# Order edges on TensorE and ScalarE for the pieces of other stages in a selective scan

## The chip, the cores and the metric

The kernel runs on one core of a Trainium2 chip. The metric is the time of one execution in microseconds of the device. Three runs of the kernel before took 17821.96, 17850.22 and 17869.16 us; their median, 17850.22 us, is the time to compare with.

The names of the engines are those of the profile: PE is TensorE (matmuls; PEld its loads of weights), DVE is VectorE, ACT is ScalarE, POOL is GpSimd, and SP is the queue that issues the DMAs.

## The reference, cut to what matters

Four layers run one after the other on eight images of 56 x 56 positions with 128 channels, all in float32. Layers 0, 2 and 3 are deformable convolutions; the change does not touch them. Layer 1 is a "visual state space" block (SS2D). Of its forward pass this is what matters here:

```python
dt = jax.nn.softplus(dt + dt_projs_b[None, :, :, None])
A = -jnp.exp(A_logs).reshape(K, Di, N)

def step(h, t):
    dt_t, u_t, B_t, C_t = t
    h = h * jnp.exp(dt_t[..., None] * A) + (dt_t * u_t)[..., None] * B_t[:, :, None, :]
    y = jnp.einsum('bkdn,bkn->bkd', h, C_t)
    return (h, y)
...
_, ys = jax.lax.scan(step, h0, ts)
```

There are K = 4 directions (rows, columns, and both backwards), Di = 256 channels and N = 16 states per channel, and L = 3136 positions to scan. Ahead of the scan stand a layer norm, a projection, a 3 x 3 depthwise convolution with SiLU, and the projections that give dt, B and C. Behind it stand a second norm, a gate, a projection back to 128 channels and an MLP with GELU.

## The kernel before, in words

The layers run one after the other; the scan layer (class `Vss`) lies in the middle of the span. Its method `scans` writes the whole layer in one loop.

**Steps and units.** A step is one image, one direction and one quarter of the positions (784 of 3136): 8 x 4 x 4 = 128 steps, sixteen to an image. A step has 32 units: eight groups of 32 channels (`cg`) by four groups of 4 states (`sg`); a unit is a tile of 32 x 4 = 128 partitions by 784 positions. So there are 4096 units, and for each of them:

- `decay` (L1424): ACT writes dA = exp(dt * A) into PSUM. Two buffers, so a decay waits for the scan two units before it.
- `inputs` (L1434): DVE multiplies u = (dt * x) * B for three of four state groups; for the fourth POOL does it (L1430, tile `up`).
- the scan (L1537): DVE runs h = dA * h + u along the 784 positions.
- L1540: ACT keeps the last column of h for the next step.
- L1542: POOL multiplies hc = h * C, into one of six buffers.
- `add_sums` (L1456): PE sums hc over the states into `acc`, two units at a time, written three units later. `close_sums` (L1467) has ACT copy `acc` out, and `open_sums` (L1448) starts the next one.

Once per channel group, `spread` (L1418) has PE copy dt * x from SBUF into PSUM (tile `dtu`, one buffer) by a product with the identity: two matmuls, four rows in the trace. DVE's u reads it. The copy for the next group is written in the unit with sg = 1, right behind the `inputs` of sg = 2, the last reader on DVE of the old copy.

**Pieces of other stages.** Three generators are cut into pieces by `yield`, and the loop runs pieces of them between the units. `prepare` computes dt, B and C of the next step (matmuls L1324 and L1337; ACT's copies and activations L1326, L1338, L1339, L1341 and L1342; POOL's L1344 and L1346; DMAs to DRAM). It is advanced as `ready`, one piece in the units with sg = 1 and 2, just before the scan of that unit is written. `output_stage` (norm, gate, projection, MLP: L1244 to L1302) and `input_stage` of the next image (stats, norm, transposes L1149, convolution L1171 and L1178, SiLU L1181) wait in the deque `tasks`, and `advance(1)` runs one piece of the first of them at the end of each unit with sg = 1, 2 or 3. In the last four steps of all it runs one in every unit. All these stages share one PSUM bank, the tile `misc` with one buffer.

**What sets the order.** The program is written with a planner that gives each engine its list of instructions. Each engine then runs its list in order. The planner goes by the order of writing, but where the oldest instruction cannot run yet in its own picture of time, a younger one that can is put first. An order edge (`issue_after(ins)`) says that what is written inside its block on the engine of `ins` stands behind `ins` in that engine's list. It adds no wait and no semaphore. The kernel has such an edge already in `add_sums`, behind `last_spread`, which is the last written copy of dt * x. SP's and POOL's lists get no edge from it, since an edge binds the engine of `ins` alone.

The calls of the three generators are in the loop of `scans`: `next(ready, None)` at L1533 and `advance`, defined at L1400. In the first image's first steps a third one, `first` (the input stage of image 0), is advanced by itself; the change leaves it as it is.

Of the kernel before, what the change touches and what calls it, by code (L numbers as in the profile page):

```python
# [44 lines left out]
AF = mybir.ActivationFunctionType  # L45
# [73 lines left out]
SC, SR = 784, 14  # L119
# [14 lines left out]
NCG, NSG = DI // TC, NST // TS  # L134
# [898 lines left out]
class Vss:  # L1033
# [339 lines left out]
    def scans(self):  # L1373
        nc, w = self.nc, self.w
# [10 lines left out]
        def chunks_for(c):  # L1385
            return min(NLC, -(-SR * (c + 1) // RPC))
# [10 lines left out]
                self.fetch_row(state[0], x, g)  # L1397
        tasks = deque()

        def advance(count):  # L1400
            for _ in range(count):
                while tasks:
                    try:
                        next(tasks[0])
                        break
                    except StopIteration:
                        tasks.popleft()

        def on_pool(t):

            return order[t][1] == NSG - 1

        def spread(at, t):

            s, (cg, sg) = state[at], order[t]
            ps = s["dtu", cg] = self.pdtu.tile([128, 2, 512], F32, name="dtu", tag="dtu")
            for b in range(2):
                last = nc.tensor.matmul(ps[:, b, :SH], lhsT=self.net.ident, rhs=s["dt", cg][:, 1, SH * b : SH * (b + 1)], start=True, stop=True)  # L1418
            self.last_spread = last.ins

        def decay(at, t):
            (i, k, c), s, (cg, sg) = steps[at], state[at], order[t]
            da = s["dA", t] = self.pda.tile([128, 1024], F32, name="dA", tag="dA")
            nc.scalar.activation(da[:, :SC], s["dt", cg][:, 0], AF.Exp, scale=w["A"][:, k, NSG * cg + sg : NSG * cg + sg + 1])  # L1424

        def inputs(at, t):
            s, (cg, sg) = state[at], order[t]
            if on_pool(t):
                u = self.work.tile([128, SC], F32, name="up", tag="up", bufs=1)
                nc.gpsimd.tensor_mul(u, s["dt", cg][:, 1], s["b", sg])  # L1430
            else:
                u = self.work.tile([128, SC], F32, name="u", tag="u", bufs=2)
                halves = [v.rearrange("p (x e) -> p x e", x=2) for v in (u, s["b", sg])]
                nc.vector.tensor_mul(halves[0], s["dtu", cg][:, :, :SH], halves[1])  # L1434
            s["u", t] = u
# [40 lines left out]

        spread(*units[0])
        decay(*units[0])
        inputs(*units[0])
        st = ready = None  # L1480
        group, late = [], deque()
        zeros = self.zeros()
        for now, (at, t) in enumerate(units):
            (i, k, c), s, (cg, sg) = steps[at], state[at], order[t]
            forward = k < 2
            if t == 0:
                if at % NSC == 0:
                    st = self.prep.tile([128, NT], F32, name="st", tag="st", bufs=2)
                    nc.gpsimd.memset(st, 0.0)
                if at % (NDIR * NSC) == 0 and i + 1 < self.images:  # L1490
                    tasks.append(self.input_stage(i + 1))
                ready = iter(())
                early = at + 1 < NSC
                if at + 1 == NSC:
                    for _ in first:
                        pass
                if at + 1 < len(steps):
                    if steps[at + 1][0] > i:
                        self.load_xb(i + 1)
                    ready = self.prepare(state[at + 1], *steps[at + 1][1:])  # L1500
            if t % (2 * NSG) == 0:
                late.append((now + 5, open_sums, (at, t)))
            while late and late[0][0] <= now:
                _, do, args = late.popleft()
                do(*args)
            if sg == 1:
                to = divmod(NCG * at + cg + 2, NCG)
                if to[0] < len(steps):
                    self.fetch_dt(state[to[0]], to[1])
            if t in (3, 19):  # L1510
                next(zeros, None)

            for x, when in enumerate(((25, 28, 29, 30), (26, 29, 30, 31))):
                if t in when and at + 1 < len(steps):
                    self.fetch_row(state[at + 1], x, when.index(t))
            if now + 1 < len(units):
                decay(*units[now + 1])
                if not on_pool(units[now + 1][1]):
                    inputs(*units[now + 1])

                if sg == NSG - 3 and now + 3 < len(units):
                    spread(*units[now + 3])
            if now + 2 < len(units) and on_pool(units[now + 2][1]):
                inputs(*units[now + 2])
            if early and t < 16:
                for _ in range(3):
                    if self.made < chunks_for(c + 1):
                        next(first)
            if early and t == 15:
                while self.made < chunks_for(c + 1):  # L1530
                    next(first)
            if t >= 16 if early else sg in (1, 2):
                next(ready, None)  # L1533
            hh = self.work.tile([128, SC], F32, name="h", tag="h", bufs=3)
            step = 1 if forward else -1
            u, dA = s.pop(("u", t)), s.pop(("dA", t))
            nc.vector.tensor_tensor_scan(hh[:, ::step], dA[:, :SC][:, ::step], u[:, ::step], st[:, t : t + 1], ALU.mult, ALU.add)  # L1537
            if c != (NSC - 1 if forward else 0):
                last = SC - 1 if forward else 0
                nc.scalar.copy(st[:, t : t + 1], hh[:, last : last + 1])  # L1540
            hc = self.work.tile([128, SC], F32, name="hc", tag="hc", bufs=6)
            nc.gpsimd.tensor_mul(hc, hh, s["c", sg])  # L1542
            group.append((order[t], hc))
            if t % 2:
                late.append((now + 3, add_sums, (at, group)))
                group = []
                if t % (2 * NSG) == 2 * NSG - 1:
                    late.append((now + 5, close_sums, (at, t)))
            if not early and sg or (i == self.images - 1 and k == 2):
                advance(1)  # L1550
# [4 lines left out]
        while tasks:  # L1555
            advance(1)
# [82 lines left out]
```

## Time and profile before

| | us |
|---|---|
| median of three runs | 17850.22 |
| the profiled execution | 17839.74 |
| its span, first to last instruction | 17838.2 |
| scan stage, first to last scan | 2213 to 13404 |
| DVE busy, whole span | 15386.3 (86%) |
| PE busy, whole span | 13881.5 (78%) |
| POOL busy, whole span | 11758.9 (66%) |
| ACT busy, whole span | 10928.2 (61%) |
| PE's mean granted clock | 0.851 |

The groups of instructions of the scan stage that matter, each with count, busy time and mean: the scans are 3072 + 1024 with 5579.2 + 1876.7 us (1840 and 1833 ns each); hc on POOL 4096 with 7539.5 us (1874 ns); dA on ACT 4096 with 3741.9 us (915 ns); u on DVE 3072 with 2864.6 us (957 ns); the copies dtu on PE 4096 rows with 2028.2 us.

How to read it: a busy time is a sum over the whole span, where the scan stage stands between two stages with other limits, so it has to be read for that stretch alone. In the lists of waits a row says who waited for whom, with us in total, number of times, and the longest. In a timeline a row has its start, its duration, engine, line, operation, tiles (out <- in) and how many like instructions were merged; the brackets have the idle time of that engine before it, and what ended it. Matmuls in float32 leave two rows each.

### The profile page before, as it was taken

To read this page: it belongs to the slowest core of one execution; us is meant where nothing else is said; L and a number is where in the kernel's file an instruction comes from. 1 tells how busy PE (TensorE), PEld (TensorE's weight loads), DVE (VectorE), ACT (ScalarE), POOL (GpSimd) and SP (SyncE) were. 2 spreads that over 40 slices of the span, in tenths; PEclk is the share of its full clock that TensorE was granted. 3 is DMA by queue.
4 is the path that set the end of the run, shared out by engine and by line. 5 is a ranking of instruction groups with operands and counts; after the bars stand their busy time and mean duration, and the time that the engine had idled before them with its cause. 6 is when DMAs were issued, how large, how long until landed. Compare 5 with 4: busy or idle time off the path is not lost. (4 is left out here: it accounts for less than half of the span.)

```text
span 17838.2 us, 255485 instructions
## 1 busy us (share of the span) xinstructions
PE 13881.5 (78%) x90058; PEld 6881.4 (39%) x90058; DVE 15386.3 (86%) x17779; ACT 10928.2 (61%) x19607; POOL 11758.9 (66%) x6462
## 2 busy tenths in 40 slices
PE   5777788788788788788778878878776888777777
PEld 3555522232232233232223223223224666555555
DVE  8888488998998998998898899899996888888886
ACT  4666566566566566566666656656554666666666
POOL 2222189998998998998998999899992111122221
PEclk7788898899899899889888888989887888777778
DMA  7777544444343343343444344344434777777777
GB/s 211 211 204 206 165 153 154 172 169 150 143 159 141 139 163 137 139 165 137 143 162 143 137 158 144 140 155 150 148 134 134 199 198 199 196 210 193 209 196 176
DMA packets 1343087, 2961.69 MB, mean 166 GB/s; under 512 B 90960, under 2 KB 893716, under 8 KB 1327420
## 3 DMA queue, kind: packets, MB, share of 16 engines
q1 hardware_dynamic: 1341788, 2945.17, 52.9%
q8 instruction: 718, 11.76, 0.3%
q14 instruction: 581, 4.76, 0.1%
HBM read 2240.63 MB, written 866.92 MB: 174 GB/s over the span
## 5 line engine op out<-in xcount | busy, mean ns | idle before, releaser
L1542 POOL TENSOR_TENSOR hc<-h,c 128x784 f32<-128x784 f32 x4096 | 7539.5, 1874 | 640.9 <-DVE h L1537 387.9
L1537 DVE TENSOR_TENSOR_SCAN h<-dA,st,u 128x784 f32<-128x784 f32 x3072 | 5579.2, 1840 | 438.9 <-ACT dA L1424 243.2
L1424 ACT ACTIVATE dA<-dt,v_A 128x784 f32<-128x784 f32 x4096 | 3741.9, 915 | 842.2 <-DVE h L1537 827.7
L1456 PE MATMUL acc<-hc,v_sum 128*32 128x392 f32 x16384 | 3148.3, 542 | 103.9 <-POOL hc L1542 103.3
L1434 DVE TENSOR_TENSOR u<-dtu,b 128x784 f32<-128x784 f32 x3072 | 2864.6, 957 | 382.5 <-PE dtu L1418 378.4
L1418 PE MATMUL dtu<-dt,ident 128*128 128x392 f32 x4096 | 2028.2, 626 | 1081.9 <-issue 833.4
L760 POOL TENSOR_TENSOR ay<-hat,om 112x756 f32<-112x756 f32 (+2 forms) x192 | 504.6, 2628 | 2848.6 <-ACT hat L751 2309.7
L1537 DVE TENSOR_TENSOR_SCAN h<-dA,st,up 128x784 f32<-128x784 f32 x1024 | 1876.7, 1833 | 232.0 <-POOL hc L1542 208.6
L1430 POOL TENSOR_TENSOR up<-dt,b 128x784 f32<-128x784 f32 x1024 | 1908.1, 1863 | 79.5 <-DVE h L1537 47.1
L845 ACT COPY st<-pt 128x448 f32<-128x448 f32 (+1 forms) x2240 | 1177.4, 542 | 1201.1 <-PE pt L843 1194.6
L812 DVE TENSOR_TENSOR win<-win,patch 112x252 f32 (+2 forms) x3456 | 1686.4, 501 | 132.2 <-POOL win L803 32.5
L1540 ACT COPY st<-h 128x1 f32<-128x1 f32 x3072 | 582.6, 190 | 1985.3 <-DVE h L1537 1976.8
L843 PE MATMUL pt<-ident,sw 112*128 112x112 f32 (+2 forms) x8960 | 1600.6, 308 | 165.6 <-DMA sw<-skew 165.5
L1456 PEld LDWEIGHTS acc<-hc,v_sum 128*32 128x32 f32 x16384 | 762.0, 116 | 2485.3 <-issue 1656.6
L1418 PEld LDWEIGHTS dtu<-dt,ident 128*128 128x128 f32 x4096 | 860.1, 230 | 2150.6 <-issue 1365.5
L803 POOL MEMSET win<- 128x1820 f32 (+2 forms) x384 | 630.0, 1647 | 1298.4 <-DMA skew<-win 1111.2
L859 PE MATMUL yps<-st,xw 128*32 128x48 f32 (+5 forms) x35840 | 1075.2, 244 | 420.7 <-ACT st L845 414.6
L843 PEld LDWEIGHTS pt<-ident,sw 112*128 112x128 f32 (+2 forms) x8960 | 1113.4, 160 | 441.0 <-issue 156.8
L809 DVE TENSOR_TENSOR patch<-ay,hat 112x756 f32<-112x756 f32 (+2 forms) x1152 | 1225.3, 1070 | 39.5 <-POOL ay L760 36.6
L859 PEld LDWEIGHTS yps<-st,xw 128*32 128x32 f32 (+2 forms) x35840 | 754.1, 125 | 849.5 <-ACT st L845 501.0
L749 ACT ACTIVATE hat<-om,taps 112x252 f32<-112x252 f32 x1280 | 758.6, 730 | 277.2 <-DVE patch L809 261.4
L1448 PE MATMUL acc<-y,ident 128*64 128x392 f32 x1536 | 599.1, 780 | 348.6 <-ACT y L1467 269.5
(193 smaller groups left out, 19827.3 us busy)
## 6 DMA issues: line engine op xcount, KB each, us to landing
dt<-dds SPq DMA_DIRECT2D x1024, 784.0 KB
b<-rows SPq DMA_DIRECT2D x512, 392.0 KB
c<-rows SPq DMA_DIRECT2D x512, 392.0 KB
dds<-dd SPq DMA_DIRECT2D x256, 784.0 KB
sw<-skew SPq DMA_DIRECT2D x224, 812.0 KB
sw<-skew SPq DMA_DIRECT2D x224, 672.0 KB
sw<-skew SPq DMA_DIRECT2D x224, 588.0 KB
skew<-win SPq DMA_DIRECT2D x128, 560.0 KB
```

The costliest lines, as they stand in the source:

```text
L809: nc.vector.tensor_mul(patch[:n], bcast(a, 3, KX), bcast(b, 2, KY))
L812: self.last_add = nc.vector.tensor_add(to, to, patch[:n, NCB * p : NCB * (p + 1)]).ins
L843: last = nc.tensor.transpose(ps[:m, n * g : n * (g + 1)], sw[:n, g, p : p + m], self.net.ident[:n, :n])
L845: nc.scalar.copy(st[:m], ps[:m, : G * n])
L859: self.nc.tensor.matmul(yps[CG * g : CG * (g + 1), t0:t1], lhsT=xw[:m, k + part, CG * g : CG * (g + 1)], rhs=st[:m, at + t0 : at + t1], st ...
L1418: last = nc.tensor.matmul(ps[:, b, :SH], lhsT=self.net.ident, rhs=s["dt", cg][:, 1, SH * b : SH * (b + 1)], start=True, stop=True)
L1424: nc.scalar.activation(da[:, :SC], s["dt", cg][:, 0], AF.Exp, scale=w["A"][:, k, NSG * cg + sg : NSG * cg + sg + 1])
L1430: nc.gpsimd.tensor_mul(u, s["dt", cg][:, 1], s["b", sg])
L1434: nc.vector.tensor_mul(halves[0], s["dtu", cg][:, :, :SH], halves[1])
L1456: nc.tensor.matmul(acc[r : r + TC, :SH], lhsT=w["sum"], rhs=hc[:, SH * b : SH * (b + 1)], start=False, stop=sg == NSG - 1)
L1537: nc.vector.tensor_tensor_scan(hh[:, ::step], dA[:, :SC][:, ::step], u[:, ::step], st[:, t : t + 1], ALU.mult, ALU.add)
L1542: nc.gpsimd.tensor_mul(hc, hh, s["c", sg])
```

## The change

The pieces from `ready` and from `tasks` are now run inside two nested order edges, through a helper `behind`. What a piece writes on PE is put behind the copy of dt * x that was written last, and what it writes on ACT is put behind the decay that was written last; `decay` keeps that instruction for it. At sg = 1 the last written copy is the one of the next channel group, and the last written decay is that of the next unit. The loop in `advance` is rewritten to the same effect: an exhausted generator is dropped and the next one tried. What the pieces write on DVE, POOL and SP is bound by neither edge.

```diff
+        def behind(stream):
+            with self.tc.issue_after(self.last_spread), self.tc.issue_after(self.last_decay):
+                return next(stream, self)
+
         def advance(count):
             for _ in range(count):
-                while tasks:
-                    try:
-                        next(tasks[0])
-                        break
-                    except StopIteration:
-                        tasks.popleft()
+                while tasks and behind(tasks[0]) is self:
+                    tasks.popleft()
 
         def on_pool(t):
 
@@ -1421,7 +1421,7 @@
         def decay(at, t):
             (i, k, c), s, (cg, sg) = steps[at], state[at], order[t]
             da = s["dA", t] = self.pda.tile([128, 1024], F32, name="dA", tag="dA")
-            nc.scalar.activation(da[:, :SC], s["dt", cg][:, 0], AF.Exp, scale=w["A"][:, k, NSG * cg + sg : NSG * cg + sg + 1])
+            self.last_decay = nc.scalar.activation(da[:, :SC], s["dt", cg][:, 0], AF.Exp, scale=w["A"][:, k, NSG * cg + sg : NSG * cg + sg + 1]).ins
 
@@ -1530,7 +1530,7 @@
             if t >= 16 if early else sg in (1, 2):
-                next(ready, None)
+                behind(ready)
```

## The prediction

> **What bounds the kernel now.** First the windows of the span, cut at the first and the last scan. The change touches only the scan stage, from 2213 to 13404 us:
>
> ```profile
> 0.00:2213.00 2213.00, 1566.87 (x17883) 1176.05 (x17884) 1667.33 (x3408) 1290.00 (x2418) 408.50 (x239) 0.79 0.72 199
> 2213.00:13404.00 11191.00, 8898.43 (x31778) 3154.45 (x31778) 10148.66 (x7689) 6904.84 (x12124) 10440.65 (x5770) 0.89 0.42 149
> 13404.00:17839.00 4435.00, 3416.22 (x40401) 2550.93 (x40397) 3570.33 (x6683) 2733.38 (x5067) 909.79 (x454) 0.79 0.72 192
> ```
>
> The columns are the length, then busy us of PE, PEld, DVE, ACT and POOL, then the granted clock, DMA share and GB/s. In the middle row POOL is busy 93%, DVE 91%, PE 80%, ACT 62%: two engines are close to full, and 1042 us of DVE is idle. The list of waits of DVE in that stretch says what ended the idle time:
>
> ```profile
> DVE u L1434 <- PE dtu L1418: 378.4, 154, 48.6
> DVE h L1537 <- POOL hc L1542: 287.1, 261, 3.4
> DVE h L1537 <- ACT dA L1424: 246.2, 245, 5.0
> ```
>
> The change aims at rows one and three: 378 + 246 = 625 us, 3.5% of the span, is the most that two punctual producers could give. How much of it comes from a piece that stands too early in a queue is the question; two timelines show the kinds. On PE, the longest waits for dtu look like this one:
>
> ```profile
> 8233.81 5.05 PE L1171 MATMUL misc<-xn,v_tap 128*128 128x448 f32 x12
> 8238.79 0.85 PE L1456 MATMUL acc<-hc,v_sum 128*32 128x392 f32 x2
> 8239.56 1.58 PE L1418 MATMUL dtu<-dt,ident 128*128 128x392 f32 x4
> ...
> 8241.18 1.85 DVE L1434 TENSOR_TENSOR u<-dtu,b 128x784 f32<-128x784 f32 x2 [5.85 <-PE dtu L1418]
> ```
>
> Twelve rows of the input stage's convolution hold the copy up until DVE waits 5.85 us. But the code writes these matmuls before that copy, so no edge is drawn between them. On ACT, a piece that is too early:
>
> ```profile
> 5869.09 1.62 PE L1324 MATMUL misc<-xb,v_xproj 128*40 128x392 f32 x2
> ...
> 5870.74 0.48 ACT L1326 COPY dbl<-misc 40x392 f32<-40x392 f32 x1 [3.90 <-PE misc L1324]
> 5871.13 0.19 ACT L1540 COPY st<-h 128x1 f32<-128x1 f32 x1
> 5871.22 0.91 ACT L1424 ACTIVATE dA<-dt,v_A 128x784 f32<-128x784 f32 x1
> ...
> 5872.22 1.85 DVE L1537 TENSOR_TENSOR_SCAN h<-dA,st,u 128x784 f32<-128x784 f32 x1 [2.21 <-ACT dA L1424]
> ```
>
> The copy of dbl is written behind these decays and stands ahead of them; ACT waits 3.90 us at it for PE, and the scan loses 2.21 us.
>
> **The change part by part.** No instruction or DMA is added or removed; SP and POOL get no edge. What moves is the order on PE and ACT. I set the order of the instructions in the trace against the order in which the code writes them. Of the pieces from `ready` and `tasks`, 549 + 1132 matmul instructions stand on PE ahead of the copy that was written last before them, and 670 + 481 instructions on ACT ahead of such a decay. These alone are bound.
>
> *Edge on PE.* For each of 1023 copies I took the time from the end of the u that frees dtu to the end of the copy and summed what PE did in it. Pieces in the wrong order hold up 214 copies by 328 us in all, but DVE waits at only some of them, 22 us together: after the last u of a channel group DVE still has three scans (3 x 1.84 = 5.5 us) and the copy takes 1.5, so about 4 us are free. The 355 us of pieces that lie in the copies DVE does wait for stand in the written order. Gain 0 to 22 us.
>
> *Edge on ACT.* The same sum from the end of the scan that frees a decay's PSUM buffer: early pieces, run or waited for, hold up 295 decays by 280 us, and scans wait 37 us of it. Gain 0 to 37 us.
>
> Together 0 to 59; I take 30. The piece is not gone: the copy of dbl stands one decay later and still waits for its matmul at the head of ACT, and the next decay has only 0.9 us of slack (a scan of 1.84 less a decay of 0.92).
>
> *Levelling of `prepare`.* The largest displacements are of `prepare`: its L1324 stands a median of 69 us ahead of its copy, up to 263, a step being 79 to 100 us. Steps 9 to 13 of image 2 (images and steps counted from 0) show it, in the windows of the second product of `prepare` (L1346) alone; the columns are length, POOL busy us and count:
>
> ```profile
> 5855.10:5946.50 91.40, 4.47 (x2) 0.84 0.41 146
> 5946.50:6032.80 86.30, 8.32 (x4) 0.84 0.36 129
> 6032.80:6114.60 81.80, 3.71 (x2) 0.83 0.43 152
> 6114.60:6193.20 78.60, 0.00 (x0) 0.83 0.35 126
> 6193.20:6276.40 83.20, 3.71 (x2) 0.90 0.44 160
> ```
>
> Step 10 carries two prepares, step 12 none. With the edges each carries its own. Steps 10 to 12 sum to 246.7, and POOL is 100% busy in the first two, so three equal steps of 82 give nothing. Step 9 holds doubled matmuls (16 rows of L1324 where others have 8) beside the output stage, and DVE waits 6.4 us for dA and 3.3 for dtu in it; other steps with an output stage take 84. So 0 to 6 us per image, I take 5, for seven images 35. The last image, whose prepares run ahead from step 6 on, has steps of 88.1 and 87.2 against a level of about 82: 8 more. Sum 43; at most 7 x 6 + 11 = 53, and at worst a loss of 24, if step 12 rises to 82 in seven images and nothing falls.
>
> *What the new order puts behind.* A copy that waits for u now holds whatever was allowed past it: output-stage matmuls (L1285, L1297, L1262, L1264), transposes L1149, `prepare`'s, and behind these ACT's reads of `misc`, which is one bank: who holds it stops every other piece. The add_sums behind the copy free hc, for which POOL already waits 231 us. PE stands idle before a copy in 469 cases for 1051 us already, until a u ends. Upper end: the transposes feed the convolution, and if each of its 49 chunks in seven images comes late enough to make one more wait like the 5.85 above, 287 us. Lower end 0: most steps have the 4 us. The nearest row is that convolution matmuls themselves are hardly displaced (13 of 882), so I stay near the low end: one more wait of mean size (330 us without the first wait of 48.6, by 153: 2.2 us), per image, 15 us. On ACT the moved pieces are a median of under 1 us and follow the decay, where 1.8 us of each unit are free (11191/4096 = 2.73, less 0.92); cover gone, that is the stall above again.
>
> [...]
>
> **Sum.** -30 - 43 + 15 = -58 us. The profiled execution took 17839.74 (span 17838.2), so it would take 17,782; the median of the runs, 17,850.22, lies 10.5 above it, so I forecast 17,792.
>
> **The rivals.** About 0.3% (53 us) is what a measurement of this kernel can tell from no change; the three runs lie 47 apart.
>
> *A, no effect that can be told (17,797 to 17,903).* The long waits stand in the written order, POOL is 97 to 100% busy in eight of sixteen steps, and the levelled prepare costs where it saves. For it: only 22 of 330 us at dtu are from early pieces. Against: five steps per image change for certain.
>
> *B, slower.* Early pieces hurt little (22 us), late ones much (355 us), because a late piece is older than the next copy and goes first. If the edges turn early pieces into late ones in the six steps per image that hold the input stage (steps 3 to 8, 89 to 101 us against 84), each such step gets one more wait; at 3.1 us (the commonest of the long ones) to 5.85, on 6 x 7 = 42 steps, that is 130 to 246 us, less the 73 of gain: 17,907 to 18,023. It decides from 24 such waits on, where 3.1 us each eat the 73. For it: `misc` is one bank, PE is 82 to 90% busy in those steps. Against: pieces there already run two to four units later than written, so most edges bind nothing.
>
> *C, much faster.* Pieces that start right behind a copy have the whole 10.9 us (four units) until the next one, so the lumps of convolution come into phase too. If half of the 330 and 246 us goes, 288: 17,562. For it: only the phase of the lumps makes the waits. Against: nothing keeps a lump of 12 rows out of the way of the next copy.
>
> **How the numbers follow.** Forecast case 0.42 (own range 17,730 to 17,830, four fifths of its chance beyond 0.3%), A 0.22, B 0.30, C 0.06. Faster 0.34 + 0.06 = 0.40; same 0.08 + 0.22 = 0.30; slower 0.30. The range goes from 17,690, which leaves C out, to 17,940, which takes in the lower half of B and leaves out 0.12.
>
> **What would show it.** In the changed profile no L1326 or L1338 stands ahead of a decay written before it, and L1346 runs twice in each step but the last of all. The wait of the scan for dA falls from 246 to about 200; that of u for dtu moves by less than 30. Steps 9 to 13 take 416 instead of 421 us. If the wait of u for dtu rises above 420, or POOL's wait for PE's acc above 300, B is right. I am wrong if the steps with the convolution (3 to 8) change by more than 2 us each, in either direction: the order there would then have been remade by edges that I take for idle.

## The result, and the profile after

The changed kernel takes 17913.45 us (median of six runs, 17901.44 to 17933.17), the kernel before beside it 17841.35 us (six runs, 17819.69 to 17869.16). The ratio is 1.0041, with a 95% interval of 1.0028 to 1.0054: slower by 72 us. The forecast was 17,792, faster by 0.3%. The direction was wrong; the measured time lies inside the range, in the part that rival B had brought in.

Where the time came from is first read in the windows of the changed kernel, cut at its own first and last scan (length, busy us of PE, PEld, DVE, ACT and POOL, clock, DMA share, GB/s):

```profile
0.00:2213.00 2213.00, 1576.36 (x17889) 1180.38 (x17889) 1668.57 (x3408) 1290.90 (x2421) 406.53 (x240) 0.79 0.72 199
2213.00:13470.00 11257.00, 8956.48 (x31775) 3112.01 (x31776) 10143.58 (x7689) 6894.05 (x12121) 10461.80 (x5770) 0.90 0.42 148
13470.00:17902.50 4432.50, 3413.35 (x40399) 2552.55 (x40395) 3572.16 (x6683) 2731.52 (x5066) 911.23 (x454) 0.79 0.72 192
```

Ahead of the scan stage and behind it the stretches are as long as before (2213 and 4432.5 us, against 2213 and 4435). The scan stage, from its first scan to the end of its last, went from 11187.5 to 11255.7 us, so it holds all of the loss. DVE, the engine with the scans, has the same work in it (10148.66 before, 10143.58 now); what grew is its idle time. The waits of DVE in that stretch of the changed kernel (us in total, times, longest):

```profile
DVE u L1434 <- PE dtu L1418: 524.5, 193, 48.5
DVE h L1537 <- ACT dA L1424: 270.1, 234, 4.0
DVE h L1537 <- POOL hc L1542: 223.9, 196, 3.3
```

The two waits that the change aims at rose, that for dtu by 146 us (378.4 before) and that for dA by 24 (246.2). The wait for hc fell by 63. POOL's own row in the same stretch:

```profile
POOL hc L1542 <- PE acc L1456: 299.7, 179, 5.0
```

Before it was 230.9 us. The prediction gave two signs for rival B, and either was to do: the wait for dtu above 420 us, which it is, and POOL's wait for `acc` above 300, which it misses by a hair.

To place the loss, the scans were cut into steps (32 scans each) and the step times averaged over images 1 to 6. These are sums per image, in us, over three kinds of steps: those with an output stage only, those with the input stage, and those with `prepare` alone and what is left. Each row comes from one profiled execution, which need not lie at its kernel's median: that of `prepare` only lies 27 us above it, that of the smaller pieces without edges 31. The rows below the second belong to the experiments that follow.

| kernel | steps 13 to 2 | steps 3 to 8 | steps 9 to 12 | sum |
|---|---|---|---|---|
| before | 503.5 | 563.9 | 336.9 | 1404.3 |
| after | 505.6 | 574.1 | 332.0 | 1411.7 |
| edges on `prepare` only | 514.9 | 559.7 | 332.1 | 1406.7 |
| edges on the input stage only | 505.1 | 572.9 | 336.2 | 1414.2 |
| PE edge on the output stage only | 498.7 | 558.4 | 333.8 | 1390.9 |
| no edge, smaller pieces | 504.2 | 539.0 | 338.3 | 1381.5 |
| all edges, smaller pieces | 505.0 | 539.1 | 335.2 | 1379.3 |

From before to after: +2.1 in steps 13 to 2, +10.2 in steps 3 to 8, -4.9 in steps 9 to 12, so 6 x 7.4 = 44 us in six images; image 0 adds 15 and image 7 adds 9. That makes the 68 us of the stage. The two waits do not move alike: per image, u's wait for dtu rises by 10.9 us in steps 13 to 2 and by 7.0 in steps 3 to 8 (from 38.0 to 45.0), while the scan's wait for dA falls by 6.7 in the first and rises by 6.4 in the second (from 14.5 to 20.9). The 10.2 us of steps 3 to 8 thus stand at both.

The longest wait for dtu in one of these steps shows the first kind. The timeline of the changed kernel in step 6 of image 3:

```profile
7028.82 0.93 PE L1418 MATMUL dtu<-dt,ident 128*128 128x392 f32 x2
...
7029.58 4.67 PE L1171 MATMUL misc<-xn,v_tap 128*128 128x448 f32 x12
...
7034.09 0.82 PE L1418 MATMUL dtu<-dt,ident 128*128 128x392 f32 x2
...
7034.95 1.86 DVE L1434 TENSOR_TENSOR u<-dtu,b 128x784 f32<-128x784 f32 x2 [7.04 <-PE dtu L1418]
...
7037.21 0.64 ACT L1174 ACTIVATE pre<-misc,v_col 128x448 f32<-128x448 f32 x1 [7.40 <-PE misc L1171]
```

Two pieces of the convolution, twelve rows, stand between the halves of a copy. No edge forbids it: they were written before that copy. In the kernel before, u waits 3.2 us for dtu in step 6 on average, now 12.3.

### The profile page after: what moved, and what is told of

It is laid out like the page before. It is cut to its first block, busy times and chain, and to the rows that moved or that the text cites. A ratio compares the mean times of both kernels' runs of the same rounds, so it can differ in the third digit from the quotient of the medians.

```text
span 17902.5 us, 255375 instructions
## 1 busy us (share of the span) xinstructions
PE 13946.2 (78%) x90058; PEld 6844.9 (38%) x90058; DVE 15384.3 (86%) x17779; ACT 10916.5 (61%) x19607; POOL 11779.6 (66%) x6462
## 4 chain that ended last, share of the span: by engine, by line
PE 34%; DVE 18%; issue 15%; ACT 10%; POOL 9%; DMA 2%; DVEq 0%; SPq 0%; POOLq 0%; ACTq 0%
DVE h L1537 9%; PE acc L1456 7%; POOL hc L1542 6%; PE dtu L1418 5%; DVE u L1434 3%; PE misc L1171 3%; PE pt L843 2%; PE ps L902 2%; PE misc L1324 2%; PE acc L1448 2%; PE yps L859 2%; PE ps L911 2%; ACT hat L749 2%; DVE win L812 1%; ACT dA L1424 1%
## 5 line engine op out<-in xcount | busy, mean ns | idle before, releaser
L1456 PE MATMUL acc<-hc,v_sum 128*32 128x392 f32 x16384 | 3400.8, 539 | 98.3 <-POOL hc L1542 97.8
L1434 DVE TENSOR_TENSOR u<-dtu,b 128x784 f32<-128x784 f32 x3072 | 2865.6, 957 | 530.4 <-PE dtu L1418 524.5
L1418 PE MATMUL dtu<-dt,ident 128*128 128x392 f32 x4096 | 1982.1, 611 | 1453.8 <-issue 1327.3
L1418 PEld LDWEIGHTS dtu<-dt,ident 128*128 128x128 f32 x4096 | 823.7, 223 | 2529.7 <-issue 2017.6
```

The source lines that it names most:

```text
L1456: nc.tensor.matmul(acc[r : r + TC, :SH], lhsT=w["sum"], rhs=hc[:, SH * b : SH * (b + 1)], start=False, stop=sg == NSG - 1)
```

## The experiments

All of them use the helper of the change, with one or both edges, and differ in which generators go through it:

```diff
+        def behind(stream):
+            with self.tc.issue_after(self.last_spread), self.tc.issue_after(self.last_decay):
+                return next(stream, self)
```

Times are medians, differences are against the kernel before as measured beside each run, and intervals are of the ratio.

### Which edge, and which caller

PE's edge alone and ACT's edge alone, on all pieces:

```diff
-            with self.tc.issue_after(self.last_spread), self.tc.issue_after(self.last_decay):
+            with self.tc.issue_after(self.last_spread):
```
```diff
-            with self.tc.issue_after(self.last_spread), self.tc.issue_after(self.last_decay):
+            with self.tc.issue_after(self.last_decay):
```

> Only the edge on PE is left (behind the last written copy of dt * x), for prepare and tasks alike. Theory P (the PE edge turns early pieces into late ones, which the next copy then has to wait behind): all of the loss stays, 17,890 to 17,930, and u's wait for dtu stays above 450 us (524 with both edges, 378 before). Theory Q (the ACT edge holds the one bank misc until behind a decay, and that makes the pieces late): nearly nothing is lost, 17,820 to 17,860, and the wait for dtu falls back to 380 to 420.

> Only the edge on ACT is left (behind the last written decay). Theory P: no loss; the prepares of steps 9 to 12 are still levelled, since ACT reads every matmul of prepare, so about 30 us are won: 17,800 to 17,840, and u's wait for dtu is 330 to 400 us. Theory Q: the loss stays, 17,890 to 17,930, with the wait for dtu above 450.

Both edges, but on `prepare` alone, and on the deque `tasks` alone:

```diff
-                while tasks and behind(tasks[0]) is self:
+                while tasks and next(tasks[0], self) is self:
```
```diff
-                behind(ready)
+                next(ready, None)
```

> Both edges, but only around prepare; the pieces of tasks go as before. If the pieces of tasks (transposes, convolution, output stage) that are made late are what costs, this keeps the levelling of steps 9 to 12 (-5 us per image in the changed kernel) without the loss in steps 5 and 6: 17,790 to 17,840. If prepare's own pieces do it, it is slow like the changed kernel, 17,880 to 17,930.

> Both edges, but only around the pieces of tasks; prepare runs as far ahead as before. If the pieces of tasks made late cost it: 17,900 to 17,960 (the loss of steps 5 and 6 without the 35 us that the levelling saves). If prepare's do: 17,830 to 17,860.

| run | us | difference | ratio |
|---|---|---|---|
| PE edge, all pieces | 17881.09 | +33 | 1.0015 (1.0006 to 1.0024) |
| ACT edge, all pieces | 17840.94 | -7 | 0.9995 (0.9986 to 1.0004) |
| both, `prepare` only | 17850.58 | +3 | 1.0002 (0.9993 to 1.0011) |
| both, `tasks` only | 17868.91 | +21 | 1.0009 (1.0000 to 1.0018) |

None of the four times lies in a band that had been expected. PE's edge costs, ACT's edge does nothing that can be told. By its waits PE's edge alone does what theory P says: u's wait for dtu is 520.0 us in the stage (378.4 before, 524.5 with both edges). ACT's edge does do what the prediction says of it: without the first wait of the stage, the scan's wait for dA falls from 265 to 211 us and u's wait for dtu rises from 330 to 401, the two counted with the short stalls too. One wait went and another came. The parts do not add up to the whole: +33 - 7 and +3 + 21 are both about 25, and the whole is 60 to 72. That an edge changes the planner's list as a whole is the likely reason; it was not shown.

`prepare` alone shows the levelling: -4.8 us per image in steps 9 to 12, as in the changed kernel, and -4.2 in steps 3 to 8, but +11.4 in steps 13 to 2. There the pieces that used to run a step ahead now stand among the output stage's, and u waits 13.9 us per image for dtu (1.1 before). The changed kernel has this wait too, in step 0 of image 2:

```profile
5116.39 1.51 PE L1266 MATMUL misc<-yin,v_out 128*128 128x392 f32 x4
...
5117.94 0.48 ACT L1268 COPY x<-misc 128x392 f32<-128x392 f32 x1 [2.82 <-PE misc L1266]
...
5118.61 0.93 PE L1273 MATMUL misc<-x,v_center 128*128 128x392 f32 x2
...
5120.25 1.58 PE L1418 MATMUL dtu<-dt,ident 128*128 128x392 f32 x4
...
5121.87 0.97 DVE L1434 TENSOR_TENSOR u<-dtu,b 128x784 f32<-128x784 f32 x1 [3.20 <-PE dtu L1418]
```

The copy stands behind L1273, which needs ACT's L1268, which needs PE's L1266: a round trip between two engines stands in PE's list ahead of the copy. All three are the output stage's; yet with PE's edge on that stage alone (below) the wait is 2.7 us per image in these steps, so it takes `prepare`'s edges to bring it. How they do it was not followed. Steps 0 to 2 and 13 to 15 of the kernel before had 0.1 to 0.3 us of wait for dtu each, now they have 1.6 to 2.2.

### The two generators in `tasks` apart

First the changed kernel once more, then both edges on `output_stage` alone, then on `input_stage` alone. From here on `ready` goes without edges unless it is said:

```diff
-                while tasks and behind(tasks[0]) is self:
+                while tasks and (behind(tasks[0]) if tasks[0].__name__ == "output_stage" else next(tasks[0], self)) is self:
```

> The changed kernel itself once more, beside the variants and on their chip, since the sum of PE edge alone (+33 us) and ACT edge alone (-7 us) is far from the +72 of both. If the two edges add up, 17,865 to 17,885 here; if they make each other worse, 17,900 to 17,930.

> Both edges, only around the pieces of output_stage; input_stage and prepare as before. By the steps of the run with edges on tasks only, the steps that hold nothing but the output stage (13 to 15 and 0 to 2 of the next image) became 4.8 us per image shorter, and those of the input stage 8 us longer. If each is the work of its own stage's edges: 17,800 to 17,830, u's wait for dtu 320 to 360 us. If the two can't be told apart: 17,850 to 17,880.

> Both edges, only around the pieces of input_stage. If the loss in steps 5 and 6 comes from the input stage's own pieces (transposes and norm made late, so that the convolution comes in lumps at the next copy): 17,890 to 17,920, with steps 5 and 6 at 98 to 104 us against 95. If it comes from the output stage's pieces running on into them: 17,840 to 17,860.

And a choice made from the step times so far, with the output stage's edges always, those of `prepare` in steps 3 to 12, none for the input stage:

```diff
-                behind(ready)
+                behind(ready) if 3 <= at % (NDIR * NSC) <= 12 else next(ready, None)
```

> Edges only where the steps became shorter: output_stage always, prepare in steps 3 to 12 of each image, input_stage never. Per image -4.8 us in steps 13 to 2 (as with tasks only), -4.2 in steps 3 to 8 and -4.8 in 9 to 12 (as with prepare only), over some seven images, if these parts add: 17,745 to 17,790. If a change of order in one step class spoils the next: 17,830 to 17,870.

| run | us | difference | ratio |
|---|---|---|---|
| the changed kernel again | 17901.77 | +60 | 1.0038 (1.0024 to 1.0051) |
| output stage only | 17773.39 | -69 | 0.9962 (0.9948 to 0.9976) |
| input stage only | 17897.17 | +55 | 1.0031 (1.0019 to 1.0043) |
| chosen | 17783.44 | -59 | 0.9969 (0.9957 to 0.9981) |

This is the main result of the study: edges on single stages have effects of opposite sign, each as large as the forecast. The output stage's edges gain 69 us (more than had been expected), the input stage's lose 55 (in the band of the theory that blames its own pieces). They do not explain the whole by addition: -69 + 55 is -14 where both in `tasks` took +21, and with the +3 of `prepare` the parts make -11, where the change costs 60 to 72. In steps 3 to 8 the three parts sum to about -1 us per image (-4.2, +9.0, -5.5 with PE's edge alone on the output stage) and the whole to +10.2. So some 70 to 80 us of the change's cost (each part is known to 16 to 25 us) come only with the edges together, and their cause stays open. The changed kernel again lies in the band for edges that make each other worse. The chosen kernel lies in its expected band (17,745 to 17,790) but is no better than the output stage's edges alone, so `prepare`'s edges added nothing to it: they level steps 9 to 12, and the time comes back elsewhere.

### What the output stage's edge gains

PE's edge alone, on the output stage alone:

> The PE edge alone, only around output_stage. Of that stage no ACT instruction stood ahead of an earlier written decay before, so the PE edge should make the whole gain of the two (-69 us): 17,760 to 17,790. If the ACT edge has part in it, 17,800 to 17,850.

It took 17762.52 us, -74 us, ratio 0.9956 (0.9943 to 0.9970). All of the output stage's gain is the edge on PE, for which the prediction allowed 22 us at most. In the whole stage DVE's wait for dtu, the only place where the prediction had looked, falls by 11 us (378.4 to 367.5: by 29 in images 1 to 6, of which images 0 and 7 give 19 back), the scan's wait for dA by 25 (246.2 to 221.6), and that of the input stage's statistics for a DMA by 13 (28.4 to 15.5). So part of the path goes elsewhere. The kernel before, step 14 of image 2:

```profile
6303.35 1.51 PE L1244 MATMUL misc<-yin,v_off 128*128 128x392 f32 x2
...
6304.66 1.42 PE L1244 MATMUL misc<-yin,v_mid 128*128 128x392 f32 x2
...
6306.01 1.51 PE L1456 MATMUL acc<-hc,v_sum 128*32 128x392 f32 x8
6306.12 0.49 ACT L1245 COPY yc<-misc 128x392 f32<-128x392 f32 x1 [1.80 <-PE misc L1244]
...
6307.57 0.48 ACT L1467 COPY out<-acc 64x392 f32<-64x392 f32 x1 [0.87 <-PE acc L1456]
...
6309.22 0.91 ACT L1424 ACTIVATE dA<-dt,v_A 128x784 f32<-128x784 f32 x1
...
6310.23 1.85 DVE L1537 TENSOR_TENSOR_SCAN h<-dA,st,u 128x784 f32<-128x784 f32 x1 [1.49 <-ACT dA L1424]
```

L1244 of the output stage stands ahead of the `add_sums`. So PE's sums are late, ACT stands 1.80 us at L1245 and 0.87 us at L1467 (`close_sums`, written behind the sums), and the decay behind them on ACT starts at 6309.22, although its buffer was free since the scan that started at 6302.41 had ended, at 6304.23. The scan waits 1.49 us for ACT by the trace, and ACT in turn had waited for a place in PE's list. The decay thus starts 5.0 us after its buffer had come free, and ACT is idle for 2.67 us of them. The same place with PE's edge on the output stage:

```profile
6277.48 1.51 PE L1456 MATMUL acc<-hc,v_sum 128*32 128x392 f32 x8
...
6279.11 0.93 PE L1244 MATMUL misc<-yin,v_off 128*128 128x392 f32 x2
...
6280.91 0.47 ACT L1245 COPY yc<-misc 128x392 f32<-128x392 f32 x1
6281.41 0.48 ACT L1467 COPY out<-acc 64x392 f32<-64x392 f32 x1
...
6282.56 0.90 ACT L1424 ACTIVATE dA<-dt,v_A 128x784 f32<-128x784 f32 x1
...
6283.56 1.85 DVE L1537 TENSOR_TENSOR_SCAN h<-dA,st,u 128x784 f32<-128x784 f32 x1 [0.28 <-ACT dA L1424]
```

The sums go first, ACT waits at neither copy, and the scan loses 0.28 us in place of 1.49. In the waits of ACT over the scan stage the chain has its own rows; before:

```profile
ACT y L1467 <- PE acc L1456: 323.7, 229, 3.1
...
ACT out L1467 <- PE acc L1456: 110.1, 77, 3.1
...
ACT yc L1245 <- PE misc L1244: 60.7, 42, 3.7
```

and with PE's edge on the output stage:

```profile
ACT y L1467 <- PE acc L1456: 216.5, 151, 3.1
...
ACT out L1467 <- PE acc L1456: 59.2, 54, 2.9
...
ACT yc L1245 <- PE misc L1244: 13.2, 12, 3.7
```

Per step and image, step 0 falls from 5.7 to 0.1 us of ACT waiting for `acc` and from 1.9 to 0.3 us of the scan waiting for dA; step 14 from 5.2 to 0.1 and from 2.2 to 0.4. By the table of steps this gains 4.8 us per image in steps 13 to 2, some 29 us in six images. Step 3, which holds pieces of both stages, gains another 4.8 (its waits for dtu, for dA and for a DMA all shrink); the 3.1 in steps 9 to 12 were not followed. The chain is thus shown for about a third of the gain.

How the edge does it is only partly known. It sets L1244 against the copy, not against the sums, which are written behind L1244 here; and in the kernel before none of the 256 matmuls of L1244 stands ahead of the copy that was written last before it. Other matmuls of the output stage do: 115 of 128 of L1262, 224 of 256 of L1264, 100 of 256 of L1285. With them bound, the planner's list came out with the sums ahead of L1244, which no edge asks for.

In the changed kernel the same chain is cut: its step 0 has 0.1 us of ACT waiting for `acc` and 0.3 of the scan for dA. But its wait for dtu there went from 0.3 to 2.1 us, by the round trip shown above. The gain was made, and spent on the copy.

### What the input stage's edges lose

ACT's edge alone and PE's edge alone on the input stage, and both edges on it but not on the pieces of its norm (statistics and z, which go without an edge):

```diff
-                while tasks and behind(tasks[0]) is self:
+                while tasks and (behind(tasks[0]) if tasks[0].__name__ == "input_stage" and not self.norm else next(tasks[0], self)) is self:
```

> The ACT edge alone, only around input_stage. Theory N (the norm: its four rs, two more small ones and four z activations, some 3 us of ACT per chunk, ran up to 60 us ahead in ACT's idle time and now stand between decays, beside SiLU and its two table loads): the loss of both edges on this stage stays, 17,880 to 17,910, the scan's wait for dA at 285 us or more. Theory T (the PE edge: transposes late, convolution in lumps before the next copy): 17,835 to 17,860.

> The PE edge alone, only around input_stage. Theory N: no loss, 17,835 to 17,860, dA near 265. Theory T: 17,880 to 17,910, with u's wait for dtu at 370 us or more (330 before).

> Both edges around input_stage, except around its two pieces that hold the norm (stats, and z). Theory N: loss gone, 17,835 to 17,860, steps 5 to 7 back to 291 us together (299 with the edges on the whole stage). Theory T: loss stays, 17,880 to 17,910.

| run | us | difference | ratio |
|---|---|---|---|
| ACT edge, input stage | 17875.59 | +39 | 1.0020 (1.0011 to 1.0029) |
| PE edge, input stage | 17875.36 | +38 | 1.0019 (1.0010 to 1.0028) |
| both, without the norm's pieces | 17862.57 | +25 | 1.0014 (1.0005 to 1.0023) |

Either edge loses about 38 us by itself, which lies between the bands of the two theories. By the waits both have a part: ACT's edge raises the scan's wait for dA from 265 to 287 us, PE's edge raises u's wait for dtu, again without the stage's first, from 330 to 360 (370 or more had been expected). Without the norm's pieces 25 us are left (9 to 41 by the interval) of the 55, again between the bands, and steps 5 to 7 take 297.4 us together where 291 were expected; so the norm is a part of the loss, and its share is not well known. Before the change the norm of a chunk ran far ahead of where it was written (at the median 41 us for z, some 90 for its statistics). With the edges it comes next to the SiLU and its two loads of tables. From the kernel with both edges on the input stage, step 6 of image 2, ACT and the scan:

```profile
5669.83 0.59 ACT L1339 ACTIVATE dd<-misc,v_col 128x392 f32<-128x392 f32 x1 [2.37 <-DMA dds<-dd]
...
5671.25 0.84 ACT L1132 ACTIVATE bn_rs<-bn_mv,bn_rs 112x1 f32<-112x1 f32 x4
5671.41 1.85 DVE L1537 TENSOR_TENSOR_SCAN h<-dA,st,u 128x784 f32<-128x784 f32 x1 [3.92 <-ACT dA L1424]
...
5674.24 1.65 ACT L1139 ACTIVATE z<-xt,bn_rs 112x128 f32<-112x128 f32 x4
...
5675.79 0.90 ACT L1424 ACTIVATE dA<-dt,v_A 128x784 f32<-128x784 f32 x1
...
5676.79 1.85 DVE L1537 TENSOR_TENSOR_SCAN h<-dA,st,u 128x784 f32<-128x784 f32 x1 [2.52 <-ACT dA L1424]
```

The norm's 0.84 + 1.65 us stand ahead of a decay that has 0.9 us of slack. The first 3.92 us come from what ACT did just before: two loads of tables (1.28 us each) around a SiLU of 1.70, and 2.37 us at L1339 for a buffer that a DMA still read. On PE the transposes L1149 (164 of 196 of which used to run ahead of the copy written before them, by 4.1 us at the median) now come behind it, and the convolution that needs them comes later after a copy: a lump of twelve or more rows (other matmuls may stand between its rows, but no copy) started 1.4 us after the end of the copy at the median, and starts 3.2 us after it in the changed kernel.

### Whether it is the size of the lumps

A late piece is one written before the next copy, so no edge keeps it out of that copy's way; if that is what costs, its price is its length. In the next three kernels the convolution computes three of its nine taps (another output), so a lump is a third as long. The first has no edge, the others PE's or ACT's edge on the input stage.

```diff
-                for tap in range(9):
+                for tap in (0, 3, 6):
...
-                    if tap % 3 == 2 and tap < 8:
+                    if tap < 6:
```

> The kernel before with the convolution cut to three of its nine taps (one matmul per piece in place of three; the output is another, and the pieces are as many as before). A yardstick for the next two. The input stage's steps (4 to 7) lose their lumps of 12 and 18 rows on PE; u waited 140 us for dtu in such intervals in six images, so with seven images some 160 to 300 us less: 17,550 to 17,690.

> The same cut, with the PE edge around input_stage (which cost 38 us with nine taps). If the edge costs because the convolution's lumps start later behind a copy (median 3.1 us against 1.4) and run into the next one, the loss is gone without lumps: -15 to +15 us against the cut kernel without edges. If the cost has nothing to do with the lumps: +25 to +50.

> The same cut, with the ACT edge around input_stage (which also cost 38 us). If this edge costs through ACT's own time (the norm between the decays): +20 to +50 us against the cut kernel without edges. If it costs through late lumps as well: -15 to +15.

Against the kernel before, 17837.13 us, they took 17530.17 (0.9828, 0.9811 to 0.9844), 17566.58 (0.9844, 0.9827 to 0.9860) and 17580.73 (0.9858, 0.9842 to 0.9875). The first is the yardstick, and 20 us below its band. With a third of the convolution's matmuls PE's edge on the input stage still costs 36 us (by its four runs against four, 36 ± 27), where 15 at most was expected if lumps were the cause. ACT's edge costs 50 (52 ± 16). That theory fell for the input stage's edge by itself. The loss still stands at the same two waits: with PE's edge, in steps 3 to 8 and per image, u's wait for dtu goes from 15.0 to 21.4 us and the scan's for dA from 5.8 to 9.3.

The other way round, with the whole convolution and its pieces cut at two taps instead of three (four rows in place of six, and five pieces of a product in place of three, so that the stage also spreads over more units):

```diff
-                    if tap % 3 == 2 and tap < 8:
+                    if tap % 2 == 1:
```

with PE's edge on the output stage, with no edge at all, and in the changed kernel:

> The PE edge around output_stage alone (-74 us), with the convolution cut into pieces of two taps in place of three (five pieces per convolution, all nine taps). If the size of a lump sets u's wait for dtu in the input stage's steps, lumps of 8 rows in place of 12 let 40 to 100 us more go: 17,660 to 17,725. If late pieces merge into lumps whatever their size, 17,750 to 17,780.

> No edges at all, only the convolution's pieces of two taps in place of three. The run with the output stage's edge on TensorE and these pieces took 17,639, the one with that edge alone 17,762.5: 124 us for the small pieces if the two gains lie in different steps of an image and add. Then this kernel takes 17,837 - 124 = 17,713 (17,695 to 17,730), with the gain in steps 3 to 8 and steps 0 to 2 and 13 to 15 as before. If the small pieces only help once the output stage's matmuls are out of the way, it takes 17,760 or more.

> The changed kernel with all its edges, and the convolution's pieces of two taps. If the changed kernel loses because its late pieces are lumps of convolution ahead of the next copy, the shorter lumps give back more here than the 124 us of the other pair: 17,740 or less. If the loss is in the order of the input stage's other pieces, as the runs with three taps say, the small pieces give the same 124 (100 to 140): 17,765 to 17,805, and the loss against the kernel with small pieces alone stays 60 to 80.

| run | us | difference | ratio |
|---|---|---|---|
| smaller pieces, PE edge on the output stage | 17639.11 | -198 | 0.9886 (0.9870 to 0.9903) |
| smaller pieces alone | 17665.03 | -180 | 0.9895 (0.9879 to 0.9912) |
| smaller pieces, all edges of the change | 17688.16 | -157 | 0.9907 (0.9891 to 0.9924) |

All three beat both kernels. The first two are faster than had been expected (the smaller pieces alone gain 180 us where 124 had been worked out), and the third lies in the band of the lumps, 17,740 or less. The table of steps has its place: steps 3 to 8 go from 563.9 to 539.0 us per image. The gain is not at the copy, where the runs had been expected to show it: u's wait for dtu is as before, and the scan's wait for hc falls. The smaller pieces alone:

```profile
DVE u L1434 <- PE dtu L1418: 376.2, 197, 48.6
...
DVE h L1537 <- POOL hc L1542: 168.8, 171, 3.2
```

Before, these were 378.4 and 287.1 us. Behind the second stands POOL's own wait for PE's sums, which free its buffers: 111.1 us, 230.9 before. By these waits it is the `add_sums` that the smaller pieces let through on PE, in steps 3 to 8 above all, where the scan's wait for hc goes from 21.6 to 6.0 us per image. Whether their length does it or that the stage spreads over more units was not separated.

The output stage's edge adds only 18 us to it by the differences (26 by the medians, 30 ± 29 by the runs, which come from two chips), not 74: the two gains do not add.

The difference between the second and the third row is what the change costs once the pieces are small: 23 us (17 ± 28), where it was 60 to 72. And the table has the sum of steps 3 to 8 at 539.0 and 539.1: the 10.2 us per image that the change cost there are gone. So in the change as a whole that part of the loss goes with the smaller pieces, while with three taps the input stage's edges still cost 6.8 and 8.5 us in the same steps (523.6 to 530.4 and 532.1). The theory of the lumps, which fell there, fits the times here. These two readings do not fit one cause, and what else the input stage's edges cost stays open. A cancellation is not excluded either: edges on `prepare` and on the output stage alone shorten these steps by 4.2 and 5.5 us, and no run has the input stage's edges alone with the smaller pieces. Nor do the late pieces vanish: u's wait for dtu in the third row is 492.6 us in the stage, 116 more than in the second. A second PSUM bank for `misc`, which would show whether the one bank makes pieces late, was not tried.

## Why the prediction was wrong, point by point

**The bound.** That only the scan stage moves held. What was missed is that the waits for dtu and dA were read as two producers with a cause each: the wait for dA was put down to ACT, and the edge on PE was priced by u's wait for dtu alone. The wait between them in the list, that for hc, was left aside, and the smaller pieces gained there.

**Edge on PE, 0 to 22 us.** Too small, and looked for in the wrong place. On the output stage alone the edge gains 74 us, while the stage's wait for dtu falls by 11. Some 29 us of it are the chain above: L1244 ahead of the sums, L1467 at the head of ACT, the decay behind it. The forecast's sums over the copies also count overlapping rows twice (twelve rows of the convolution, 0.54 us each, take 4.67 us together): with each moment counted once, its 355 us are about 250.

**Edge on ACT, 0 to 37 us.** With that edge alone the wait for dA falls by 54 us, more than the 37 allowed. The price was missing: u's wait rises by 71, and the time stays.

**Levelling of `prepare`, 43 us.** The levelling came as told, the gain did not. In the windows of the changed kernel for L1346 alone, steps 9 to 13 of image 2, each step has its two:

```profile
5890.90:5978.80 87.90, 4.55 (x2) 0.90 0.40 142
5978.80:6061.90 83.10, 4.51 (x2) 0.77 0.38 134
6061.90:6142.80 80.90, 3.70 (x2) 0.81 0.40 141
6142.80:6224.10 81.30, 3.70 (x2) 0.79 0.40 144
6224.10:6307.50 83.40, 3.70 (x2) 0.92 0.46 162
```

They sum to 416.6 us against 421.3 before; forecast was 416. Over images 1 to 6 it is 4.9 us each in steps 9 to 12, 29 us. The 8 us of the last image came as well, in the two steps named: 88.1 and 87.2 became 83.4 and 83.1. But its steps 3 and 4 went up by 4.1 and 7.1 us and its steps 10 to 12 by 8.7 together, so the image as a whole lost 9. With the edges on `prepare` alone the same steps 3 and 4 take 88.9 and 88.8 us (84.1 and 85.3 before), and the kernel as a whole is 3 us off the one before (0.9993 to 1.0011): by itself this term of the sum measured +3, not -43. The levelled work costs where it is put.

**PE's idle time before the copies.** The prediction has 1051 us of it and in its sum no term for more. The row of the copies in the changed kernel's list of groups (busy us and mean ns, then the idle time before them):

```profile
L1418 PE MATMUL dtu<-dt,ident 128*128 128x392 f32 x4096 | 1982.1, 611 | 1453.8 <-issue 1327.3
```

PE stands idle before the copies for 1454 us, 372 more than before (1082). But the copies took 1982.1 us in all, 46 less than before, and the granted clock of the stage went from 0.89 to 0.90. The copies after more than 3.5 us of idle time became more, 182 in place of 94, and as slow as those were (988 ns against 992 for the first of a copy's four rows, 885 against 892 over all four); those after under 1 us became faster, from 575 to 526 ns per row over all four. What sets the time of a row was not shown.

**What the new order puts behind, 15 us.** This is the step that failed and that decided. It was set at one more wait of 2.2 us per image, on the ground that convolution matmuls themselves are hardly displaced; u's wait for dtu rose by 146 us. Of these, 73 lie in steps 3 to 8. There the convolution need not be displaced: what feeds it (norm and transposes) was, and it came late with that. Another 84 lie in steps 13 to 2, at output-stage matmuls, which the prediction named and gave no price (steps 9 to 12 gave 10 back). And where the cover is gone on ACT, which had no price either, the scan's wait for dA rose by 6.4 us per image in steps 3 to 8. The sum that the prediction made over 1023 copies, made again on the changed kernel: pieces ahead of their order held copies up by 328 us and now by 0, as promised by the edges; pieces in the written order by 561 us and now by 977; and in the copies that DVE does wait for, these pieces make up 359 (355 in the prediction) and now 704 us (about 250 and 485 with each moment counted once). The edges did not take pieces out of the copies' way, they turned early ones into late ones. Without the levelled steps 9 to 12 the images lost 6 x (2.1 + 10.2) + 15 = 89 us, where the forecast had 15 less 30 of direct gain; with 29 us back from the levelling and the 9 of the last image that is, but for rounding, the 68 of the stage. The upper bound of 287 did hold it. Which step failed is thus shown; how much of the cost belongs to which edge is not, since the parts do not add.

**The rivals.** B was right in its mechanism: early pieces made late, and late ones older than the next copy. Steps 3, 5 and 6 moved by more than the 2 us that were to tell (-2.8, +4.4 and +9.9). Its price was too high: the steps with the input stage were to lose 130 to 246 us in seven images and lost 61 in images 1 to 6 and 7 in image 0. The argument against it, that pieces there already run later than written, counted the convolution and not what feeds it. A had the levelling right, that it costs where it saves, but took the other edges for idle, and by stages they bind much, in both directions. Of C nothing was seen: the lumps start later after a copy, not sooner.

**What would show it.** No L1326 or L1338 stands ahead of a decay written before it any more, and L1346 runs twice per step: right. The wait for dA at about 200 and that for dtu within 30 of before: both wrong (270 and +146).

## What to carry to other kernels

An order edge does not take work out of a queue's way; it moves it to the other side of one instruction, and in front of the next. Before adding one, ask of each piece whether it is early or late now, and follow it through every engine that reads what it makes: here a matmul that went first on TensorE made a scan on VectorE wait 1.49 us for ScalarE. And try such an edge for each producer by itself and then together: here one gained 74 us and one lost 55, and all together lost 72, which is not their sum. Smaller pieces gained more than any edge, at a wait at which no edge had aimed.

## What the runs showed that was not expected

Work on an engine that is 80% busy and not the bound was far from free. Twelve rows of the convolution take 4.67 us on PE in the timeline above, so the 1344 rows that the three-tap kernel leaves out are, by an estimate from these, 1344 x 4.67 / 12 = 523 us of PE; the kernel became 307 us faster. And the same work cut into smaller pieces, with nothing left out, gave 180 us.
